# Two attention layers and two expert layers on one core: the first loads in another order, and the values' bias behind the projection of the values

## The chip, the core and the metric

The kernel runs on one core of one Trainium2 chip. What counts is the device time of one execution in microseconds (us). A core has TensorE (PE, matrix products), VectorE (DVE), ScalarE (ACT), GpSimd (POOL) and SyncE (SP, which here only issues transfers), and 16 DMA engines that serve the transfers which SP, ACT and POOL issue. Each engine works through its own list of instructions in order.

## The reference

Four sequences of 1024 tokens with 256 channels go through four residual stages:

```python
x = x + attn0(layernorm(x))   # causal, 16 heads of 16, linear position bias
x = x + ffn0(layernorm(x))    # router, 2 of 4 experts, each a full attention
x = x + attn1(layernorm(x))   # causal, rotary positions
x = x + ffn1(layernorm(x))    # 8 of 64 experts, and a shared one
...
qkv = x @ w_attn + b_attn     # in attn0
y = softmax(scores) @ v
return y @ w_proj + b_proj
```

Each row of the softmax sums to one, so the bias of v goes through it unchanged: the kernel leaves that bias out of v and adds b_v @ w_proj + b_proj, one row of 256 numbers, to x beforehand.

## The kernel before

All of x stays in SBUF, as four tiles x0 to x3 of 128 partitions x 8 x 256 floats (1 MB each; token 128 i + p lies in partition p). Everything is float32.

**The first attention** (`layer0_attn`) makes one job for each sequence and gives them to `run_attention`, which writes the order of PE, DVE and ACT out by hand, tick by tick. A job has `prepare` (the normalisation `norm`), `make_qk` (queries and keys of a group of four heads), `values` (`project_v`) and `finish`. A tick makes one step of the maxima: two score products (L282), the causal mask on the diagonal (L294) and the maximum (L297); later ticks also make a step of exponentials (L317, L328) and of products with v (L385). Between them the running parts get a turn each; that is how `values` lies among the first steps of maxima. For the first sequence `norm` comes first: 8 statistics (L76, L77), reciprocal root (L81 to L85), shift (L87), 8 row blocks on POOL (L98), 16 transposes on PE (L109), two copies on ACT (L113). Then pq and pk (L165), qa (L634) and ka (L639), which needs bk and the constant kc; then the steps of maxima begin.

**The bias** (`out_bias`): two loads on SP, bcol (1 KB, L200) and brow (128 KB, L204); a copy that spreads bcol (brep, L202); two products with wo (pbias, L207); the sum with brow (L211). `add_bias` (L217, POOL) adds the result to a whole x tile. Before, `out_bias` is called ahead of the jobs, so pbias is the first thing PE does, and `add_bias` is the last thing in `prepare`.

**The loads at the start.** SP: x0 in one transfer, gw and its second part (the last layer's gates, L1068, L1071), wq, wk, wv, wo (L593), bq, bk (L611, L612), bcol, brow, kc (L616); then `ffn_constants`: four small ones, four fills of the memory that the first expert layer gathers in (xc, 4 MB each, L690), neg (L712); then the first expert's weights and bias. ACT: x1, x2, x3. A transfer takes one of eight semaphores in turn, and SP waits, before it issues one, for the transfer that had the same semaphore. The scaling of bq (L613) stands in DVE's list ahead of the shift (L87).

Of the kernel before, what the change touches and what calls it, by code (L numbers as in the profile page):

```python
# [16 lines left out]
ALU = mybir.AluOpType  # L17
# [4 lines left out]
P = 128  # L22
B, T, C = 4, 1024, 256
# [3 lines left out]
NT = T // P  # L27
NTOK = B * T
E0 = 4
E1, TOPK, CAP = 64, 8, 128  # L30
# [14 lines left out]
class Kernel:  # L45
    def __init__(self, ctx, tc, ins, out):
        self.tc, self.nc, self.ins, self.out = tc, tc.nc, ins, out
        nc = self.nc
        self.const = ctx.enter_context(tc.tile_pool(name="const", bufs=1))
        self.xpool = ctx.enter_context(tc.tile_pool(name="x", bufs=1))  # L50
        self.npool = ctx.enter_context(tc.tile_pool(name="xnT", bufs=2))
        self.small = ctx.enter_context(tc.tile_pool(name="small", bufs=2))

        self.sent = []
        self.x = []
        self.xnT_of = {}
        for b in range(B):
            t = self.xpool.tile([P, NT, C], F32, tag=f"x{b}", name=f"x{b}")
            queue = nc.scalar if b else nc.sync
            queue.dma_start(out=t, in_=ins["x"][b].rearrange("(i p) c -> p i c", p=P))  # L60
            self.x.append(t)
        self.ident = self.const.tile([P, P], F32, tag="ident", name="ident")
        make_identity(nc, self.ident)
        self.z = self.const.tile([P, NTOK // P], F32, tag="z", name="z")

# [534 lines left out]
    def layer0_attn(self):  # L602
        tc, nc, ins = self.tc, self.nc, self.ins
        wp, rp = self.w1, self.r1
        wq = self.load_w(wp, "wq", ins["a_wq"], 512)
        wk = self.load_w(wp, "wk", ins["a_wk"], 512)
        wv = self.load_w(wp, "wv", ins["a_wv"], C)
        wo = self.load_w(wp, "wo", ins["a_wo"], C)
        bq = rp.tile([P, NG], F32, tag="a_bq", name="bq")
        bk = rp.tile([P, NG], F32, tag="a_bk", name="bk")  # L610
        nc.sync.dma_start(out=bq, in_=ins["a_bq"])  # L611
        nc.sync.dma_start(out=bk, in_=ins["a_bk"])  # L612
        nc.vector.tensor_scalar(bq, bq, 0.25, None, ALU.mult)  # L613
        bias = self.out_bias(rp, "a_bias", ins["a_bv"], ins["a_bo"], wo)
        kc = self.p2.tile([P, T], F32, tag="kc", name="kc")
        nc.sync.dma_start(out=kc, in_=ins["pos_rows"])  # L616
        self.ffn_constants()
        jobs = []
        for b in range(B):
            def prepare(job, b=b):  # L620
                yield from self.norm(b, self.ps, self.new_rows())
                job["xnT"] = self.xnT_of[b]
                self.add_bias(b, bias)

            def values(job):
                job["v"] = self.next_v()
                yield from self.project_v(wv, job["xnT"], job["v"])

            def make_qk(job, g):
                qa = self.qk.tile([P, T], F32, tag="qa", name="qa")  # L630
                ka = self.qk.tile([P, T], F32, tag="ka", name="ka")
                job["qk", g] = qa, ka
                pq = self.project(wq, g, job["xnT"], "pq")
                nc.scalar.activation(  # L634
                    qa, pq, AF.Identity, bias=bq[:, g : g + 1], scale=0.25
                )
                yield
                pk = self.project(wk, g, job["xnT"], "pk")
                nc.vector.scalar_tensor_tensor(  # L639
                    ka, pk, bk[:, g : g + 1], kc, ALU.add, ALU.add  # L640
                )
                yield

            def finish(job, b=b):
                yield from self.project_out(job["y"], wo, self.add_to_x(b))

            jobs.append(dict(n=NT, prepare=prepare, make_qk=make_qk, values=values, finish=finish))
            jobs[b]["then"] = self.route0(b) if b else self.route_and_fill()
        self.run_attention(jobs, causal=True)
# [403 lines left out]
    def open_moe(self, ctx):  # L1053
        tc, nc, ins = self.tc, self.nc, self.ins
        wp = self.moe = ctx.enter_context(tc.tile_pool(name="m1", bufs=1))
        dram = ctx.enter_context(tc.tile_pool(name="dm", bufs=1, space=DRAM))

        self.xs = [
            dram.tile([NSLOT + n * T * TOPK, XW], F32, tag=f"xs{k}", name=f"xs{k}")
            for k, n in enumerate((B - 1, 1))  # L1060
        ]

        self.sums = [
            dram.tile([(B - 1) * T + CAP, C], F32, tag=f"sum{k}", name=f"sum{k}") for k in range(2)
        ]
        self.xn_d = [dram.tile([P, 2, T], F32, tag=f"xn{b}", name=f"xn{b}") for b in range(B - 1)]
        self.gw = wp.tile([P, 2, E1 + 1], F32, tag="gw", name="gw")
        nc.sync.dma_start(  # L1068
            out=self.gw[:, :, 0:E1], in_=ins["g_w"].rearrange("(c p) e -> p c e", p=P)
        )  # L1070
        nc.sync.dma_start(  # L1071
            out=self.gw[:, :, E1 : E1 + 1], in_=ins["sg_w"].rearrange("(c p) e -> p c e", p=P)
        )
        self.before = wp.tile([P, P], F32, tag="before", name="before")
        nc.gpsimd.memset(self.before, 1.0)
        nc.gpsimd.affine_select(
            self.before, self.before, pattern=[[1, P]], compare_op=ALU.is_gt, fill=0.0, base=0,
            channel_multiplier=-1,
        )
        self.allones = wp.tile([P, P], F32, tag="allones", name="allones")  # L1080
        nc.gpsimd.memset(self.allones, 1.0)

        self.first = wp.tile([P, E1], F32, tag="first", name="first")
        nc.gpsimd.iota(
            self.first, pattern=[[CAP, E1]], base=1, channel_multiplier=0,
            allow_small_or_imprecise_dtypes=True,
        )
        self.full = wp.tile([1, 1], I32, tag="full", name="full")
        self.counts = wp.tile([P, NT + 1, E1], F32, tag="counts", name="counts")
        nc.vector.memset(self.counts[:, NT, :], 0.0)  # L1090

    def temporary(self, name):
        return self.got.tile([P, 2, C], F32, tag="g", name=name).rearrange(
            "p k c -> p (k c)"
        ).rearrange("p (i e) -> p i e", e=E1)
# [486 lines left out]
```

## Time and profile before

| | us |
|---|---|
| median of 3 runs | 4618.35 |
| the three runs | 4598.04, 4618.35, 4621.28 |
| the profiled execution | 4602.72 |
| its span | 4600.9 |
| PE busy | 4294.8 (93%) |
| DVE busy | 2601.6 (57%) |
| ACT busy | 1941.7 (42%) |
| POOL busy | 629.3 (14%) |
| x0, from issue to landing | 7.4 |
| median of a fill of xc, from issue to landing | 27.8 |

The profile follows one execution. Busy times overlap, since the engines work beside each other, so their sum is no time; what counts is which wait ends last at a place. In a line of the timeline the first number is the start, the second the duration, then come engine, line and operation, the tile written and the tiles read, and in brackets how long the engine stood idle before it and what ended that. SPq and ACTq are issues of transfers, which take time of the issuing engine and say nothing yet of the landing.

### The profile page before, as it was taken

The numbers are of one execution on the slowest core, as the hardware profiler recorded it, in microseconds if no ns is written. First come the engines' busy times: TensorE is split into PE (matmuls) and PEld (weight loads), VectorE is DVE, ScalarE is ACT, GpSimd is POOL, SyncE is SP. The second block draws the span as 40 slices with busy tenths as digits, with TensorE's granted clock in tenths as the row PEclk, the third lists the DMA queues.
The fourth block names the chain that finished last, engine by engine and source line by source line (L and its number), as shares of the span: only waits on it lengthen the run. The fifth ranks groups of instructions, "written<-read, shape, count | busy, mean of one in ns | idle before, by whom it ended". The sixth has DMA issues, their size and how long they took to land.

```text
span 4600.9 us, 85874 instructions
## 1 busy us (share of the span) xinstructions
PE 4294.8 (93%) x36762; PEld 2011.7 (44%) x36762; DVE 2601.6 (57%) x4327; ACT 1941.7 (42%) x4134; POOL 629.3 (14%) x671
## 2 busy tenths in 40 slices
PE   7999999979999998899999999998999998999998
PEld 3444444444444444544434343434334344443556
DVE  5656666636555563455465656563665766657232
ACT  2444444434555553344354555453243333334431
POOL 1002020110000000000000101010210342425243
PEclk8999999989999999999899999999899999999999
DMA  6004000010000000100000100000000111112586
GB/s 218 1 1 142 1 20 4 29 39 1 15 8 8 1 17 30 34 16 18 23 9 10 32 9 20 6 22 28 19 1 28 39 56 41 60 44 86 140 190 174
DMA packets 134443, 188.74 MB, mean 41 GB/s; under 512 B 14816, under 2 KB 116448, under 8 KB 133216
## 3 DMA queue, kind: packets, MB, share of 16 engines
q1 hardware_dynamic: 91584, 99.11, 6.9%
q0 software_dynamic: 27264, 66.18, 5.1%
q10 hardware_dynamic: 15136, 17.20, 1.1%
q8 instruction: 303, 4.96, 0.5%
q14 instruction: 156, 1.28, 0.1%
HBM read 83.36 MB, written 99.09 MB: 40 GB/s over the span
## 4 chain that ended last, share of the span: by engine, by line
PE 51%; issue 17%; DVE 5%; ACT 2%; DMA 1%; POOL 1%; another core or an unknown queue 0%; POOLq 0%; SPq 0%; DVEq 0%; ACTq 0%
PE s L282 16%; PE av L385 9%; PE s L317 6%; PE pa L165 3%; PE pb L165 2%; PE pgu L1263 2%; PE pq L165 2%; PE pk L165 2%; PE po L436 2%; PE pv L182 1%; DVE mx L297 1%; DMA xg<-xs 1%; ACT e L328 1%; PE py L403 1%; PE po L1281 1%
## 5 line engine op out<-in xcount | busy, mean ns | idle before, releaser
L328 ACT ACTIVATE e<-s 128x512 f32<-128x512 f32 (+3 forms) x3428 | 1531.0, 498 | 1829.0 <-PE s L317 1016.0
L297 DVE TENSOR_REDUCE mx<-s 128x2 f32<-128x1024 f32 (+3 forms) x1760 | 1721.8, 981 | 745.8 <-PE s L317 624.7
L317 PE MATMUL s<-qa,ka 32*128 32x384 f32 (+3 forms) x7040 | 1858.7, 552 | 24.5 <-ACT e L328 8.3
L282 PE MATMUL s<-ka,qa 32*128 32x384 f32 (+3 forms) x7040 | 1686.7, 563 | 97.0 <-DVE mx L297 38.8
L385 PE MATMUL av<-e,v 128*32 128x192 f32 (+2 forms) x12800 | 906.2, 359 | 5.6 <-ACT e L334 4.2
L282 PEld LDWEIGHTS s<-ka,qa 32*128 32x128 f32 x7040 | 556.0, 190 | 713.2 <-issue 443.4
L317 PEld LDWEIGHTS s<-qa,ka 32*128 32x128 f32 x7040 | 706.3, 186 | 131.9 <-ACT e L328 76.1
L385 PEld LDWEIGHTS av<-e,v 128*32 128x32 f32 x12800 | 266.6, 109 | 710.9 <-issue 673.0
L294 DVE TENSOR_TENSOR s<-s,mask 128x256 f32<-128x256 f32 x512 | 219.0, 428 | 205.7 <-PE s L282 197.4
L953 POOL DMA_DIRECT2D xc<-os x24 | 18.1, 754 | 2031.4 <-DVE os L949 1872.2
L1241 POOL DMA_INDIRECT xs<-rowsx,dest x192 | 185.7, 967 | 185.2 <-DVE dest L1240 163.0
L341 PEld LDWEIGHTS <-ident_b 128*32 128x32 bf16 x4096 | 62.1, 95 | 231.9 <-issue 217.4
L98 POOL TENSOR_SCALAR rows<-x,rstd,shift 128x256 f32<-128x256 f32 x96 | 51.8, 554 | 767.5 <-DVE shift L87 748.3
L403 PE MATMUL py<-ident,avs 128*128 128x128 f32 x544 | 95.9, 292 | 64.0 <-ACT avs L399 62.7
L341 PE MATMUL s<-mask_kq,ident_b 128*32 128x128 bf16 x4096 | 151.6, 228 | 0.0
L165 PE MATMUL pq<-xT,wq 128*128 128x512 f32 (+2 forms) x384 | 147.4, 522 | 2.6 <-ACT xT L920 2.5
L165 PE MATMUL pk<-xT,wk 128*128 128x512 f32 (+2 forms) x384 | 141.4, 505 | 0.1
L436 PE MATMUL po<-wo,yT 128*128 128x256 f32 x544 | 129.7, 390 | 10.6 <-ACT yT L431 10.6
L941 DVE SCALAR_TENSOR_TENSOR ka<-pk,bk,kc 128x768 f32<-128x768 f32 (+3 forms) x64 | 52.3, 818 | 149.4 <-PE pk L165 149.4
L407 DVE RECIPROCAL rec<-py 128x16 f32<-128x16 f32 (+2 forms) x160 | 38.4, 240 | 164.9 <-PE py L403 164.7
L365 DVE TENSOR_TENSOR qa<-pm,qa 128x512 f32<-128x512 f32 (+2 forms) x160 | 97.4, 609 | 52.8 <-PE pm L361 51.7
L1410 POOL DMA_INDIRECT sum<-ye,idx x64 | 100.0, 1563 | 153.7 <-DVE ye L1408 92.9
(202 smaller groups left out, 3260.0 us busy)
## 6 DMA issues: line engine op xcount, KB each, us to landing
xc<-empty SPq DMA_DIRECT2D x4, 4096.0 KB, 27.8
gu<-in_e_gu SPq DMA_DIRECT2D x64, 256.0 KB, 3.8
xs<-empty ACTq DMA_DIRECT2D x16, 642.0 KB, 6.1
xg<-xs SPq DMA_DIRECT2D x64, 160.5 KB, 3.6
dn<-in_e_dn SPq DMA_DIRECT2D x64, 128.0 KB, 2.4
sum<-sum SPq DMA_DIRECT2D x12, 512.0 KB, 4.8
rows<-xc SPq DMA_DIRECT2D x19, 256.0 KB, 3.1
xc<-os POOLq DMA_DIRECT2D x8, 512.0 KB
```

The costliest lines, as they stand in the source:

```text
L165: nc.tensor.matmul(pt[:, h, 0:wd], lhsT=w[:, c, g * P : (g + 1) * P], rhs=xnT[:, c, h * 512 : h * 512 + wd], start=(c == 0), stop=(c == 1),)
L282: nc.tensor.matmul(s[:, jj, 0:w], lhsT=qa[r : r + 32, q0 : q0 + P], rhs=ka[r : r + 32, k0 : k0 + w], start=True, stop=True,)
L294: nc.vector.tensor_tensor(d, d, self.mask.unsqueeze(1).to_broadcast([P, 2, P]), ALU.add)
L297: nc.vector.tensor_reduce(mx, s[:, :, 0:w], AX.X, ALU.max)
L317: nc.tensor.matmul(t[:, 0 : end - q0], lhsT=ka[r : r + 32, kt * P : (kt + 1) * P], rhs=qa[r : r + 32, u["q0"] + q0 : u["q0"] + end], start ...
L328: lambda e=e, t=t, jj=jj, w=end - q0: nc.scalar.activation(e[:, jj, 0:w], t[:, 0:w], AF.Exp)
L341: nc.tensor.matmul(t[j : j + 32, 0:P], lhsT=self.ident_b[:, j : j + 32], rhs=self.mask_kq, start=False, stop=True, skip_group_check=True,)
L385: nc.tensor.matmul(u["av"][32 * j : 32 * j + 32, c0:c1], lhsT=v[:, kt, c : c + 32], rhs=e[:, j % 2, c0 - q0 : c1 - q0], start=(first and h ...
L403: nc.tensor.transpose(pt[:, q].rearrange("p h r -> p (h r)"), avs[:, q * P : (q + 1) * P], self.ident)
L436: nc.tensor.matmul(po[:, q, :], lhsT=yT[:, q, c, :], rhs=wo[:, c, :], start=(c == 0), stop=(c == 1),)
L1241: d = nc.gpsimd.indirect_dma_start(out=self.xs[int(last)][:, :], out_offset=bass.IndirectOffsetOnAxis(ap=at, axis=0), in_=rows[:, i, :], i ...
L1410: nc.gpsimd.indirect_dma_start(out=of[:, :], out_offset=bass.IndirectOffsetOnAxis(ap=idx[:, 0:1], axis=0), in_=ye, in_offset=None, compute ...
```

## The change

x0 is loaded in four pieces of two row blocks each, by turns on SP and ACT; x1 to x3 are issued on SP, x1 after the attention's weights, x2 and x3 after the constants of the expert layer with their fills. bq and bk go ahead of wq and wk, kc ahead of wv and wo, the two loads of gw behind x3. The scaling of bq is in the first job's `prepare`, behind `norm`. `out_bias` is called in the first job's `values`, behind `project_v`, and its two loads are issued there; `add_bias` is there too, for every sequence. Nothing else differs in what is computed.

```diff
         for b in range(B):
             t = self.xpool.tile([P, NT, C], F32, tag=f"x{b}", name=f"x{b}")
-            queue = nc.scalar if b else nc.sync
-            queue.dma_start(out=t, in_=ins["x"][b].rearrange("(i p) c -> p i c", p=P))
+            if b == 0:
+                for r in range(0, NT, 2):
+                    queue = nc.scalar if r % 4 else nc.sync
+                    queue.dma_start(out=t[:, r : r + 2], in_=self.rows_of(b, r, 2))
             self.x.append(t)
...
+    def rows_of(self, b, i, n):
+
+        return self.ins["x"][b][i * P : (i + n) * P, :].rearrange("(i p) c -> p i c", p=P)
...
-        wq = self.load_w(wp, "wq", ins["a_wq"], 512)
-        wk = self.load_w(wp, "wk", ins["a_wk"], 512)
-        wv = self.load_w(wp, "wv", ins["a_wv"], C)
-        wo = self.load_w(wp, "wo", ins["a_wo"], C)
+
         bq = rp.tile([P, NG], F32, tag="a_bq", name="bq")
         bk = rp.tile([P, NG], F32, tag="a_bk", name="bk")
         nc.sync.dma_start(out=bq, in_=ins["a_bq"])
         nc.sync.dma_start(out=bk, in_=ins["a_bk"])
-        nc.vector.tensor_scalar(bq, bq, 0.25, None, ALU.mult)
-        bias = self.out_bias(rp, "a_bias", ins["a_bv"], ins["a_bo"], wo)
+        wq = self.load_w(wp, "wq", ins["a_wq"], 512)
+        wk = self.load_w(wp, "wk", ins["a_wk"], 512)
         kc = self.p2.tile([P, T], F32, tag="kc", name="kc")
         nc.sync.dma_start(out=kc, in_=ins["pos_rows"])
+        wv = self.load_w(wp, "wv", ins["a_wv"], C)
+        wo = self.load_w(wp, "wo", ins["a_wo"], C)
+        nc.sync.dma_start(out=self.x[1], in_=self.rows_of(1, 0, NT))
         self.ffn_constants()
-        jobs = []
+        for b in range(2, B):
+            nc.sync.dma_start(out=self.x[b], in_=self.rows_of(b, 0, NT))
+        self.load_gates()
+        jobs, biases = [], []
         for b in range(B):
             def prepare(job, b=b):
                 yield from self.norm(b, self.ps, self.new_rows())
                 job["xnT"] = self.xnT_of[b]
-                self.add_bias(b, bias)
-
-            def values(job):
+                if b == 0:
+                    nc.vector.tensor_scalar(bq, bq, 0.25, None, ALU.mult)
+
+            def values(job, b=b):
                 job["v"] = self.next_v()
                 yield from self.project_v(wv, job["xnT"], job["v"])
+                if b == 0:
+                    biases.append(self.out_bias(rp, "a_bias", ins["a_bv"], ins["a_bo"], wo))
+                self.add_bias(b, biases[0])
```

`load_gates` holds the two loads of gw that stood in `open_moe`, unchanged.

More of the change, by code (lines that the diff above doesn't have):

```diff
@@ L1067, in open_moe @@
         self.gw = wp.tile([P, 2, E1 + 1], F32, tag="gw", name="gw")
[L1068 to L1073, printed above, removed]
         self.before = wp.tile([P, P], F32, tag="before", name="before")
@@ L1090, in open_moe, with load_gates @@
         nc.vector.memset(self.counts[:, NT, :], 0.0)
+    def load_gates(self):
+        nc, ins = self.nc, self.ins
+        nc.sync.dma_start(
+            out=self.gw[:, :, 0:E1], in_=ins["g_w"].rearrange("(c p) e -> p c e", p=P)
+        )
+        nc.sync.dma_start(
+            out=self.gw[:, :, E1 : E1 + 1], in_=ins["sg_w"].rearrange("(c p) e -> p c e", p=P)
+        )
     def temporary(self, name):
```

## The prediction

> **What bounds the kernel now.** I read the page first, for the scale and for the chain that ended last; then the timeline of the first 100 us, since every edit lies there; then the transfers' issues and landings; then the table of stretches, for DMA rates and the clock.
>
> ```profile
> span 4600.9 us, 85874 instructions
> ...
> PE   7999999979999998899999999998999998999998
> ...
> DMA  6004000010000000100000100000000111112586
> ...
> PE 51%; issue 17%; DVE 5%; ACT 2%; DMA 1%; POOL 1%; another core or an unknown queue 0%; POOLq 0%; SPq 0%; DVEq 0%; ACTq 0%
> ```
>
> PE works nearly everywhere, and DMA is 1% of the chain. Only the first slice (115 us) shows PE at 7 and DMA at 6. What the change can move lies in that slice; behind it everything follows from PE's and VectorE's own order, so a shift of the start stays a shift of the end.
>
> The timeline of the start (start us, duration us, engine, line):
>
> ```profile
> 8.22 0.43 DVE L76 BATCH_NORM_STATS2 st<-x 128x6 f32<-128x256 f32 x1 [6.13 <-DMA x<-in_x]
> ...
> 16.43 0.43 SPq L200 DMA_DIRECT2D bcol<-in_a_bv  x1
> ...
> 18.94 0.17 DVE L613 TENSOR_SCALAR bq<-bq 128x4 f32<-128x4 f32 x1 [5.70 <-DMA bq<-in_a_bq]
> 19.02 0.16 DVE L87 SCALAR_TENSOR_TENSOR shift<-mv,rstd 128x8 f32<-128x8 f32 x1
> ...
> 19.29 0.32 DVE L202 COPY brep<-bcol 128x256 f32<-128x256 f32 x1
> ...
> 19.65 2.07 PE L207 MATMUL pbias<-wo,brep 128*128 128x256 f32 x4 [19.65 <-DVE brep L202]
> ...
> 20.71 34.38 SPq L690 DMA_DIRECT2D xc<-empty  x4
> ...
> 21.76 0.42 DVE L211 TENSOR_TENSOR bias<-pbias,brow 128x256 f32<-128x256 f32 x1 [2.16 <-PE pbias L207]
> ...
> 44.09 0.43 DVE L294 TENSOR_TENSOR s<-s,mask 128x256 f32<-128x256 f32 x1
> ...
> 55.13 10.67 SPq L712 DMA_DIRECT2D neg<-in_neg_rows  x1
> ```
>
> Two things. VectorE stands from 13.2 to 18.94 at the scaling of bq (L613), and the normalisation's shift is queued behind it: a true loss of the start. And once the four fills of xc are in SP's queue, SP is kept in issuing until 65.8 us.
>
> Whether a small load behind the fills gets past them:
>
> ```profile
> L690 SPq DMA_DIRECT2D xc<-empty x1: 13714/13714/13714, 41.4 to 41.4; - x1
> DMA to landing us min/median/max: 30.6/30.6/30.6
> ...
> neg<-in_neg_rows SPq DMA_DIRECT2D x1, 0.5 KB, 17.6
> ```
>
> The last fill lands at 41.4 + 30.6 = 72.0, and neg, 0.5 KB, at 55.1 + 17.6 = 72.7. It does not get past.
>
> Rates and clock (PE, PEld, DVE, ACT, POOL busy, then clock, DMA share, GB/s):
>
> ```profile
> 0.00:5.00 5.00, 0.00 (x0) 0.00 (x0) 1.08 (x3) 0.00 (x0) 4.35 (x12) 1.00 0.51 167
> 5.00:10.00 5.00, 0.00 (x0) 0.00 (x0) 1.68 (x7) 1.28 (x1) 3.72 (x13) 1.00 1.09 370
> 10.00:15.00 5.00, 0.00 (x0) 0.00 (x0) 2.80 (x13) 0.21 (x1) 0.00 (x0) 1.00 1.07 393
> ...
> 30.00:40.00 10.00, 7.79 (x35) 5.37 (x34) 3.00 (x5) 1.01 (x1) 0.00 (x0) 1.00 1.04 345
> 40.00:50.00 10.00, 8.40 (x37) 3.97 (x37) 6.48 (x10) 1.01 (x1) 0.00 (x0) 0.89 1.04 345
> 50.00:60.00 10.00, 8.26 (x30) 3.09 (x27) 6.92 (x11) 0.00 (x0) 0.00 (x0) 0.50 1.04 344
> ```
>
> Loads run at 370 to 393 GB/s, fills at 345; from the fifties on PE has half its clock.
>
> **The change, part by part.** *The front.* x0 in four pieces over two queues, with nothing of x1 to x3 beside it: x0 (1.05 MB) needs 167 x 5 = 0.84 MB up to 5 us and the rest at 370, so it is there at 5.6, plus about 0.5 to land; the first two pieces, 0.52 MB, at about 4.4. Eight pairs L76/L77 take 4.35 us (8.22 to 12.56): done at 8.8 instead of 12.6. bq now comes before wq and is scaled behind the shift, so the 5.7 us wait goes: ident_b's copy, root and reciprocal as before (0.6), shift at 9.5 instead of 19.02. Without pbias (L207) ahead of the transposes another 1.0 goes. Pool's iota ends at 8.72, wq and wk (1.05 MB behind x0) are in by 9, kc, wv and wo by 12: none is late for a first pq near 13.6. Bound: if PE's clock warms later, 2 us less. The same point in the work comes 8.5 to 10.5 us earlier; I take 10.5.
>
> *What is moved behind.* The built order of the changed kernel differs on PE by one move only: pbias now stands behind the third score step (the first group's projections, three score steps and the 16 value products are ahead of it), with the copy brep and the sum bias at that place on VectorE. Queued behind on VectorE: the mask of the fourth step, all maxima, the ka of all later groups. On PE: all scores. Nothing of either can pass. The third maximum ends near 44.0 - 10.5 = 33.5.
>
> brep waits for bcol. L200's two loads no longer stand at 16.43, before the fills, but on SP behind: four fills, neg, x2, x3, and the two loads of gw. So:
> - ahead of the fills: x0, wq, wk, kc, wv, wo, x1 = 4.19 MB. By the table 0.84 + 1.85 = 2.69 MB by 10 us, the other 1.50 at 393: 13.8. Four small loads behind x1: 1.0 (estimate; they are issued 0.47 apart now). Fills start at 14.8, were issued about 11 and so wait in the queue.
> - fills: 16.78 MB at 345 = 48.6: until 63.4.
> - x2 and x3: 2.10 MB at 380 = 5.5: 68.9.
> - gw, its second part, bcol, in small pieces: 1.2 (estimate, from wo and the small bcol behind it landing 0.2 apart to gw landing 0.9 after x0); landing: 1.4 of the 2.8 us that bcol took alone. bcol is there at 71.5.
> - Issue isn't later: neg's ends 6.2 us before the last fill lands, so near 57; x2, x3 and gw at most 4 each (the third x on ACT's queue took 3.76), bcol by 66 to 69.
>
> Bounds: 68.5 with no price for small pieces and landing, 75 if the fills get 325 GB/s.
>
> From landing to the next mask, by the rows above: bcol there 19.2, brep, pbias, bias done 22.2, so 3.0; the fourth step's two score products behind pbias add 0.3. The fourth mask stands at 44.09 now, and at 71.5 + 3.3 = 74.8 then: **+30.7**. VectorE and PE idle from 33.5 to 71.5; the 10.5 won at the front only lengthen that idling, and are worth nothing.
>
> *The clock behind the wait.* A few rows of PE:
>
> ```profile
> 46.72 1.13 PE L282 MATMUL s<-ka,qa 32*128 32x512 f32 x4 [0.42 <-DVE mx L297]
> 48.05 3.75 PE L282 MATMUL s<-ka,qa 32*128 32x512 f32 x8 [0.20 <-DVE mx L297]
> ...
> 68.40 5.28 PE L165 MATMUL pq<-xnT,wq 128*128 128x512 f32 x8
> ...
> 74.89 3.70 PE L165 MATMUL pk<-xnT,wk 128*128 128x512 f32 x8 [0.36 <-ACT qa L634]
> ```
>
> A 512-wide step goes from 1.13 to 1.88 us at 48, and full speed is back only within pq (5.28 against 3.70): some 23 us at half clock, although PE was busy 8 to 9 tenths. The Trainium skill (TensorE: Matmul & The Clock Gate, "What's actually happening") says that an idle window of about 3.4 us halves the clock and one busy window of that length restores it. After 38 us of idling both agree on a cold start. By the rule it lasts one window, about +1 us; then the steps up to pq, cold from 48 on today, would be quicker than now by about 0.45 us in each of some 13, -6: 30.7 + 0.3 + 1 - 6 = +26. By the row, score products on 32 rows do not restore it, and only pq does: then the four steps that are warm today (256, 384, 384 and 512 wide: 0.9, 1.24, 1.33, 1.33) cost 1.28, 1.57, 1.57 and 1.88 as the cold ones do: +1.5. I take the row.
>
> *The rest.* brep of the first expert stands one step later on VectorE, waiting for its bcol, 1.7 MB of weights behind: 4.8 us after ours, when VectorE arrives at 4.7. 0 to 2; I take 0.3. add_bias (4.51 us on POOL) runs near 75 instead of 24.3, with POOL idle until 197 now: nothing, hidden while x0's attention lasts. x1 is in at 14, x2 and x3 at 69, and their rows are made at 197, 326 and later; gw is used in the last layer; nothing. ACT issues two transfers less: its root waits for rstd anyway; nothing.
>
> Sum: 30.7 + 1.5 + 0.3 = **+32.5 us**. On the profiled execution's own 4602.72 (span 4600.9 and 1.8 around it) that is 4635.2. It was one of the quicker ones: the three timed runs and it have their middle at (4602.72 + 4618.35) / 2 = 4610.5. I put the sum on that: **4643**.
>
> **The rivals.**
> - *The bias' load is not held (not slower).* Were bcol's 1 KB served beside the fills, it would be there before 33.5; 10.5 won, 2.5 paid for pbias and bias at their new place: -8, 4602.5. It decides from a landing before about 62, where the loss is 23 us, 0.5%. For it: nothing but bcol's size. Against it: neg, smaller, landed 0.7 us behind the last fill, and brep's own wait cannot be passed in order. 5%.
> - *The clock comes back at once* (the rule above): +26, 4636.5. For it: the idle start is followed by PE working without gaps. Against: the same steps stayed cold for 20 us now. 20%.
> - *A longer wait*: fills at 325 GB/s (+3), the second brep 2 us late, pq and pk cold for another window (+3): +40, 4650.5. For it: two pieces of the wait are estimates. 15%.
> - The forecast: 60%.
>
> **How the numbers follow.** Apart from the first rival the cases reach from +23 (clock back at once, bcol at 68.5) to +40; runs of one kernel lie up to 12 us off their middle: 4610.5 + 23 - 12 to 4610.5 + 40 + 12 gives 4622 to 4662, which leaves out the first rival and the ends. About 0.5%, 23 us, is what a measurement of this kernel can tell from no change. Slower by more: the forecast, the longer wait, and half or more of the clock rival, less what the spread of runs takes: 0.78. Within: the first rival and the rest: 0.20. Faster: 0.02.
>
> **What would show it.** In the changed profile: shift (L93 there) near 9.5; brep (L208) on VectorE with some 38 us of idling put down to bcol, ending near 71.5; the last fill landing near 64; half clock from there to the next pq near 100; POOL's add_bias near 75; the steps behind 120 us as now, all later by one amount. It is wrong if bcol lands before the fills' end, or if the score steps behind the wait run at 1.3 us and not at 1.6 to 1.9.

## The result, and the profile after

| | before | after |
|---|---|---|
| median, us | 4616.61 (6 runs, 4598.04 to 4621.35) | 4648.93 (6 runs, 4640.81 to 4658.39) |
| the profiled execution | 4602.72, span 4600.9 | 4640.81, span 4639.1 |

The ratio after/before is 1.0076, with a 95% interval of 1.006 to 1.0091: slower by 32.3 us between the medians, where +32.5 was forecast (4643, range 4622 to 4662). The page of the changed kernel:

```profile
span 4639.1 us, 85876 instructions
...
PE   5999999979999998899999999998999999999998
...
PEclk7999999988999999999899999999899999999999
DMA  6003100000000001100000000000000111112586
...
PE 65%; DVE 5%; ACT 3%; issue 2%; DMA 2%; POOL 1%; SPq 0%; DVEq 0%; ACTq 0%; POOLq 0%
```

PE's first slice (116 us) is 5 instead of 7: about a quarter of that slice is lost there, and no other slice has lost as much. PE's rise in the chain from 51% to 65% is no loss of time: the chain now goes through PE's own work where before it put 17% down to issue, and PE's busy time grew by only 17 us (4294.8 to 4312.0).

The timeline of the start after the change (start, duration, engine, line; in brackets the idle time before and what ended it):

```profile
4.35 0.43 DVE L82 BATCH_NORM_STATS2 st<-x 128x6 f32<-128x256 f32 x1 [2.26 <-DMA x<-in_x]
...
9.41 0.17 DVE L93 SCALAR_TENSOR_TENSOR shift<-mv,rstd 128x8 f32<-128x8 f32 x1
...
34.30 0.69 DVE L303 TENSOR_REDUCE mx<-s 128x2 f32<-128x512 f32 x1
```

The front does what it says: the shift stands at 9.41 instead of 19.02. The third maximum ends at 34.99; before, it ended at 44.00 (43.31 + 0.69). Of 9.6 us won, 9.0 are left there. VectorE from there on, first in the kernel before, then in the changed one:

```profile
43.31 0.69 DVE L297 TENSOR_REDUCE mx<-s 128x2 f32<-128x512 f32 x1
...
78.63 1.28 DVE L639 SCALAR_TENSOR_TENSOR ka<-pk,bk,kc 128x1024 f32<-128x1024 f32 x1 [2.63 <-PE pk L165]
```

```profile
69.27 0.29 DVE L208 COPY brep<-bcol 128x256 f32<-128x256 f32 x1 [34.27 <-DMA bcol<-in_a_bv]
71.73 0.42 DVE L217 TENSOR_TENSOR bias<-pbias,brow 128x256 f32<-128x256 f32 x1 [2.17 <-PE pbias L213]
72.96 0.43 DVE L300 TENSOR_TENSOR s<-s,mask 128x256 f32<-128x256 f32 x1 [0.81 <-PE s L288]
...
74.37 2.58 DVE L208 COPY brep<-bcol 128x256 f32<-128x256 f32 x1
...
111.47 1.28 DVE L652 SCALAR_TENSOR_TENSOR ka<-pk,bk,kc 128x1024 f32<-128x1024 f32 x1 [2.63 <-PE pk L171]
```

One bracket holds the result: VectorE stood 34.27 us for bcol, and the fourth mask came at 72.96 instead of 44.09, **+28.9 us**. The last line is the keys of the second group, at 78.63 before: **+32.8**. Another 4.0 us were lost between the two. They begin at the second copy, which took 2.58 us where the first took 0.29.

Who waits for whom, from the table of waits of the first 120 us (sum, number, longest):

```profile
PE pbias L213 <- DVE brep L208: 35.8, 1, 35.8
DVE brep L208 <- DMA bcol<-in_a_bv: 34.3, 1, 34.3
```

PE waits for VectorE, and VectorE for the transfer. Why bcol came so late shows in the issues on SP (duration of the issue in ns, its start in us; below it the time from issue to landing), here the last fill, neg and the bias' bcol:

```profile
L703 SPq DMA_DIRECT2D xc<-empty x1: 12175/12175/12175, 32.3 to 32.3; - x1
DMA to landing us min/median/max: 30.3/30.3/30.3
...
L725 SPq DMA_DIRECT2D neg<-in_neg_rows x1: 12048/12048/12048, 44.6 to 44.6; - x1
DMA to landing us min/median/max: 18.6/18.6/18.6
...
L206 SPq DMA_DIRECT2D bcol<-in_a_bv x1: 636/636/636, 64.1 to 64.1; - x1
DMA to landing us min/median/max: 5.2/5.2/5.2
```

The last fill lands at 32.3 + 30.3 = 62.6, neg at 63.2, bcol at 69.3: one after the other, in the order of their issue. The issue of neg (0.5 KB) alone kept SP for 12 us, and bcol was not issued before 64.1. The stretches (PE, PEld, DVE, ACT, POOL busy, clock, DMA share, GB/s):

```profile
40.00:50.00 10.00, 0.00 (x0) 0.00 (x0) 0.00 (x0) 0.00 (x0) 0.00 (x0) 0.50 1.04 345
...
60.00:70.00 10.00, 0.39 (x1) 0.39 (x2) 0.29 (x1) 0.00 (x0) 0.00 (x0) 0.50 1.04 316
...
90.00:100.00 10.00, 9.27 (x28) 3.10 (x24) 7.04 (x9) 0.00 (x0) 0.00 (x0) 0.50 0.00 0
100.00:110.00 10.00, 9.64 (x20) 3.77 (x19) 2.78 (x4) 2.40 (x2) 0.00 (x0) 0.72 0.00 0
```

All five engines stand at zero while the fills flow at 345 GB/s. PE's last product ends at 33.79, the granted clock falls to half at 37.2, and it is still at half from 90 to 100, where PE is busy 9.27 of 10. Some rows of PE there, then POOL's, first in the changed kernel and then before:

```profile
74.27 1.65 PE L288 MATMUL s<-ka,qa 32*128 32x384 f32 x4 [0.98 <-DVE mx L303]
77.96 3.41 PE L288 MATMUL s<-ka,qa 32*128 32x512 f32 x8 [2.04 <-DVE mx L303]
...
100.20 6.32 PE L171 MATMUL pq<-xnT,wq 128*128 128x512 f32 x8
...
107.73 3.70 PE L171 MATMUL pk<-xnT,wk 128*128 128x512 f32 x8 [0.36 <-ACT qa L647]
```

```profile
72.30 4.50 POOL L223 TENSOR_TENSOR x<-x,bias 128x2048 f32<-128x2048 f32 x1 [57.69 <-DVE bias L217]
...
230.01 4.31 POOL L104 TENSOR_SCALAR rows<-x,rstd,shift 128x256 f32<-128x256 f32 x8 [153.22 <-DVE shift L93]
```

```profile
24.30 4.51 POOL L217 TENSOR_TENSOR x<-x,bias 128x2048 f32<-128x2048 f32 x1
197.18 4.30 POOL L98 TENSOR_SCALAR rows<-x,rstd,shift 128x256 f32<-128x256 f32 x8 [168.36 <-DVE shift L87]
```

PE is back at full speed only within pq, at 105.5. POOL's addition ends at 76.80, and the long copy on VectorE at 74.37 + 2.58 = 76.95, right behind it. The rows of the second sequence start at 230.01, 197.18 before: again +32.8. So the loss is complete by the second group and is only carried on from there. The spans differ by 38.2; the rest of 5.4 us is spread over the later stages, where matching stretches differ both ways (143.0 us at clock 0.93 before, 137.4 at 0.98 after; 2328.0 at 0.97 before, 2332.2 at 0.96 after). The medians differ by 32.3.

### The profile page after: what moved, and what is told of

It is laid out like the page before. It is cut to its first block, busy times and chain, and to the rows that moved or that the text cites. A ratio compares the mean times of both kernels' runs of the same rounds, so it can differ in the third digit from the quotient of the medians.

```text
span 4639.1 us, 85876 instructions
## 1 busy us (share of the span) xinstructions
PE 4312.0 (93%) x36762; PEld 2015.8 (43%) x36762; DVE 2603.8 (56%) x4327; ACT 1942.0 (42%) x4134; POOL 629.0 (14%) x671
## 4 chain that ended last, share of the span: by engine, by line
PE 65%; DVE 5%; ACT 3%; issue 2%; DMA 2%; POOL 1%; SPq 0%; DVEq 0%; ACTq 0%; POOLq 0%
PE s L288 21%; PE av L391 12%; PE s L323 8%; PE pq L171 3%; PE pk L171 3%; PE pa L171 3%; PE pb L171 2%; PE pv L188 2%; PE po L442 2%; PE pgu L1279 2%; DVE mx L303 2%; DMA xg<-xs 1%; PE py L409 1%; PE pm L367 1%; ACT e L334 1%
```

## The experiments

**The theory**: brep stands in order on VectorE, and its bcol is held in SP's queue behind 16.8 MB of fills. **Rivals**: any small load is slow while fills take the bandwidth, whatever its queue; the moved products and the copy cost the time at their new place; the new order of the loads costs it. A second theory followed from the after-trace: the last 4.0 us are the copy held by POOL's addition, and the cold clock. The ratios are to the kernel before on the same chip; its median was 4611.09, 4687.17, 4614.69 and 4674.71 on four of them, so medians are not compared across chips.

**1. The bias' loads first.** Two helpers, load_bcol and load_brow, hold the two loads of `out_bias`, which takes what is loaded already. Experiments 2, 3, 5, 6, 7 and 10 have them too.

```diff
         wo = self.load_w(wp, "wo", ins["a_wo"], C)
+        early = self.load_bcol(ins["a_bv"]), self.load_brow(ins["a_bo"])
...
-                    biases.append(self.out_bias(rp, "a_bias", ins["a_bv"], ins["a_bo"], wo))
+                    biases.append(self.out_bias(rp, "a_bias", ins["a_bv"], ins["a_bo"], wo, early))
```

> The changed kernel with bcol and brow loaded ahead of x1 and the fills; everything else in its order. Theory A (the loss is the wait of the copy brep for bcol, which stands in SP's queue behind the fills): brep starts near 34 us instead of 69, the fourth mask near 37; the first expert's bcol is still behind the fills (near 76) and its copy stands on VectorE where about 73 is reached, so some 3 us stay lost: about 5 us under before, 4612. Rival B (pbias and the bias at their new place, among the steps, cost the time): still 20 us or more over before. Rival C (the fills' traffic itself slows the start, wherever bcol stands): unchanged, 4649.

Measured: 4601.57 (before 4611.09), ratio 0.9979 [0.997, 0.9988]. The copies on VectorE:

```profile
33.58 0.28 DVE L219 COPY brep<-bcol 128x256 f32<-128x256 f32 x1
...
79.05 0.28 DVE L219 COPY brep<-bcol 128x256 f32<-128x256 f32 x1
```

No bracket: no wait. With the products and the first copy at the changed kernel's place, the whole loss is gone and 9.5 us are won; the keys of the second group stand at 72.04 (before 78.63). So neither the moved products nor the new order costs the time. The second copy, for which a loss of some 3 us was expected, lost nothing. It is not at the changed kernel's place: in this build it stands behind the keys of the second group in VectorE's list, as in the kernel before (80.97), well behind POOL's addition and behind its load. Its place differs from build to build: right behind the bias' sum in 2, 3, 5, 6, 7 and 10, and where the changed kernel has it, between the fifth mask and its maximum, in 4, 8, 11 and 12.

**2. The first expert's load early too.**

```diff
+        self.first_bcol = self.load_bcol(ins["f_bv"][0])
```

> As the first, with the first expert's bcol ahead of the fills too. A: no wait of VectorE for a transfer is left, about 8 us under before, 4609. B: 20 us or more over before. C: 4649.

Measured: 4604.06, ratio 0.9985 [0.9975, 0.9994]; keys of the second group at 70.97. It is no better than the first: with no second wait there was nothing to save.

**3. Bias at the front, as before, with the new order of loads.**

```diff
+        bias = self.out_bias(rp, "a_bias", ins["a_bv"], ins["a_bo"], wo)
+        self.first_bcol = self.load_bcol(ins["f_bv"][0])
...
+                self.add_bias(b, bias)
...
-                    biases.append(self.out_bias(rp, "a_bias", ins["a_bv"], ins["a_bo"], wo))
-                self.add_bias(b, biases[0])
```

> As the second, with the bias computed ahead of the jobs again, so that pbias is PE's first work: the order of the loads alone. A: about 9 us under before, 4608, within 2 us of the second. B: 9 us under before as well, but 25 us or more quicker than the second. C: 4649.

Measured: 4603.15, ratio 0.9987 [0.9979, 0.9995]. bcol's copy waited until 12.73, so pbias held the transposes until 14.95; the keys of the second group stand at 73.23, 1.2 later than in experiment 1. The intervals of 1 and 3 overlap: whether the move itself is worth that 1.2 us is not settled. One row of VectorE is worth keeping for later:

```profile
17.07 3.25 DVE L708 TENSOR_SCALAR bq<-bq 128x16 f32<-128x16 f32 x1 [1.26 <-DMA bq<-in_f_bq]
```

A scaling of 16 numbers took 3.25 us and ended at 20.32, beneath POOL's addition, 15.77 to 20.30.

**4. The bias behind the values alone**, in the kernel before, with its old order of loads.

```diff
-        bias = self.out_bias(rp, "a_bias", ins["a_bv"], ins["a_bo"], wo)
...
-                self.add_bias(b, bias)
...
+                if b == 0:
+                    biases.append(self.out_bias(rp, "a_bias", ins["a_bv"], ins["a_bo"], wo))
+                self.add_bias(b, biases[0])
```

> The kernel before, with the bias behind the projection of the values and nothing else: x0 in one piece, x1 to x3 on ACT, gw first, the old order of weights. bcol then stands behind the fills and neg. A: bcol near 73, fourth mask near 77 against 44.1, colder steps +1.5, the second copy up to 3: +36, 4652, more than the whole change. If the new order of loads were the cause: within 3 us of before, 4617. B: +20 or more, but with brep at its place near 44 and no wait for a transfer.

Measured: 4641.16, ratio 1.007 [1.0056, 1.0083]. Half of the change makes the whole loss:

```profile
70.42 0.29 DVE L202 COPY brep<-bcol 128x256 f32<-128x256 f32 x1 [26.96 <-DMA bcol<-in_a_bv]
...
77.44 1.01 DVE L202 COPY brep<-bcol 128x256 f32<-128x256 f32 x1 [1.83 <-DMA bcol<-in_f_bv]
```

The wait is 7.3 us shorter than in the changed kernel and ends within 1.2 us of the same time. This shows that the front's gain goes into the wait. (By the ratio the loss is 32 us; 36 were expected.)

**5. The loads at their new place, on ACT's queue instead of SP's.** The first expert's load is early here and in 6, 7 and 10.

```diff
+                    early = (self.load_bcol(ins["a_bv"], nc.scalar),
+                             self.load_brow(ins["a_bo"], nc.scalar))
```

> The changed kernel with bcol and brow issued at the same place of the program, near 34 us, while the fills are in full flow, but on ACT's queue; the first expert's bcol ahead of the fills, so that no second wait is left. Theory A (order within SP's queue): bcol lands some 3 to 6 us after its issue, brep near 38, fourth mask near 42, about 3 us under before, 4608. Rival C (all the DMA engines are taken by the fills, whatever the queue): brep near 65 to 70, 4640 or more.

Measured: 4684.6 (before 4687.17), ratio 1.0002 [0.9988, 1.0016]. The issue on ACT, then the copy on VectorE:

```profile
31.99 0.37 ACTq L203 DMA_DIRECT2D bcol<-in_a_bv  x1
```

```profile
37.83 0.29 DVE L219 COPY brep<-bcol 128x256 f32<-128x256 f32 x1 [4.05 <-DMA bcol<-in_a_bv]
```

Issued in the midst of the fills (338 GB/s from 30 to 40 us), bcol is used 5.8 us later. The rival of bandwidth would have it wait to the sixties. What held it was SP's queue. In the changed kernel it landed 5.2 us after its issue at 64.1, so most of its wait lay ahead of that issue; the experiment takes away SP's held issue and the place behind the fills together, and does not tell them apart. What is left, a wait of 4.05 us, takes back most of the gain.

**6. Half of the fills behind the bias' loads.**

```diff
-            nc.sync.dma_start(
-                out=self.xc[b].rearrange("(i p) c -> p i c", p=P),
-                in_=zeros.unsqueeze(1).to_broadcast([P, E0 * NT, C]),
-            )
+        self.fill_half(0)
...
                     biases.append(self.out_bias(rp, "a_bias", ins["a_bv"], ins["a_bo"], wo))
+                    self.fill_half(1)
```

> The changed kernel with half of each fill (8.4 MB of 16.8) issued behind bcol and brow, and the first expert's bcol ahead of all. A: the wait shrinks by the fills' own time, 24.3 us: brep near 45 instead of 69.3, fourth mask near 49 against 44.1 before, and PE restarts cold: 4 to 7 us over before, 4616. B (the new place costs): 20 us or more over before. C: 4645 or more.

Measured: 4697.8 (before 4687.17), ratio 1.0019 [1.0005, 1.0033], +8.9 us by the ratio.

```profile
48.47 0.29 DVE L219 COPY brep<-bcol 128x256 f32<-128x256 f32 x1 [14.01 <-DMA bcol<-in_a_bv]
```

The fourth mask comes at 52.16, +8.1. The expectation was some 3 us too low.

**7. The first expert's load early, nothing else**: `self.first_bcol` as in 2, the bias' loads as in the changed kernel.

> The changed kernel with the first expert's bcol alone ahead of the fills: the second wait of VectorE (2.3 us at 74.4 in the changed kernel's profile) taken away and the first left. A: brep still near 69.5, 2 us under the changed kernel, 30 over before, 4641. If the two waits were one cost, and the second copy the one that counts: 4610 to 4620.

Measured: 4716.63 (before 4687.17), ratio 1.0068 [1.0047, 1.0089].

```profile
71.48 0.29 DVE L219 COPY brep<-bcol 128x256 f32<-128x256 f32 x1 [37.22 <-DMA bcol<-in_a_bv]
...
74.28 0.28 DVE L219 COPY brep<-bcol 128x256 f32<-128x256 f32 x1
```

The second copy now stands just ahead of POOL's addition (74.52) and takes its 0.28 us. From the first copy to the keys of the second group it is 39.0 us (110.52), against 42.2 in the changed kernel. The medians cannot show a gain of this size: the intervals of the two ratios overlap.

**8 and 9. PE kept busy through the wait**, by 9 and 11 rounds of a projection that nobody reads, ahead of `out_bias`; one run each.

```diff
+                    for _ in range(11):
+                        self.project(wq, 0, job["xnT"], "keep")
```

> The changed kernel with 36 more projections of 128x512 on PE ahead of pbias (results unused), some 33 us that fill the wait, so that PE's clock is full when bcol comes near 69.3. The clock by the row (score steps on 32 rows lose it and do not restore it, as in the kernel before): pbias takes 1.1 instead of 2.1, the first steps run at 1.3, then half clock comes back some 24 us after the dense work's end or sooner and stays until the next pq; pq begins 1 to 3 us sooner than in the changed kernel, near 98. By the skill's rule (a busy window restores the clock, an idle one takes it): full clock for all steps, pq near 94. If the clock had no share in the loss: pq at 100.2 as before.

With 9 rounds the products ended at 64.73, PE stood 6.18 us, and pbias was cold again (2.07 us): 4730.78 on the chip of 4687.17. It tells nothing of the clock.

> As the run with 36 more projections on PE (their results unused), with 44, some 38 us, so that they end where bcol lands and leave no gap of 6 us ahead of pbias. By the row: pbias takes 1.1 instead of 2.1, one to three score steps run at full clock, then half clock until the next pq; from brep's start to the first pk some 1 to 3 us less than the 38.5 of the changed kernel. By the skill's rule: the score steps keep full clock and that stretch takes 32 us or less. If the clock had no share: 38.5.

With 11 rounds: 4642.96 on the chip of 4614.69. They reach pbias:

```profile
71.85 1.03 PE L213 MATMUL pbias<-wo,brep 128*128 128x256 f32 x4
...
76.20 1.13 PE L288 MATMUL s<-ka,qa 32*128 32x512 f32 x4 [0.42 <-DVE mx L303]
77.53 2.07 PE L288 MATMUL s<-ka,qa 32*128 32x512 f32 x4 [0.20 <-DVE mx L303]
...
98.18 5.15 PE L171 MATMUL pq<-xnT,wq 128*128 128x512 f32 x8
```

The same four products take 1.13 and, one step later, 2.07 us. The clock kept warm fell to half at 77.2, 4.4 us after pbias ended (72.88), though PE was not idle for over 1.13 us at a time; in these 4.4 us it was busy 64%. It stayed at half for 24 us, with PE busy 87% up to pq, and came back within pq, at 101.1. From the first copy to pk it is 33.6 us, against 38.5 in the changed kernel, where 1 to 3 us less were expected. Of these 4.9, 1.7 are the second copy (0.84 us here, beneath the end of POOL's addition), 1.2 are pq, which differs from run to run without such a cause (see below), and 2.0 are the warm products and steps ahead of pq.

**10. All fills behind the bias' loads.**

```diff
                     biases.append(self.out_bias(rp, "a_bias", ins["a_bv"], ins["a_bo"], wo))
+                    self.fill_half(0)
+                    self.fill_half(1)
```

> The changed kernel with all four fills issued behind bcol and brow, the first expert's bcol ahead: the bias and its loads stay where the change has put them. A: with no fill ahead bcol is there before VectorE asks for it: brep near 34 with no wait, the ratio to before 0.998 to 0.9985 as with the loads moved ahead, and on one line with half (brep 48.5) and all of the fills (71.5 on that chip) ahead. B: 0.5% over before or more. C (the fills' traffic): no gain over before either, since the same 16.8 MB flow beside the first steps.

Measured: 4605.51 (before 4614.69), ratio 0.9982 [0.9971, 0.9994].

```profile
33.67 0.28 DVE L219 COPY brep<-bcol 128x256 f32<-128x256 f32 x1
```

With 0, 8.4 and 16.8 MB of fills ahead (10, 6 and 7) the first copy stands at 33.7, 48.5 and 71.5. The fills, still running at 368 GB/s from 30 to 40 us here, disturb nothing when they are behind.

**11. The addition later**, by six empty turns ahead of `add_bias` for the first sequence.

```diff
+                    for _ in range(6):
+                        yield
                 self.add_bias(b, biases[0])
```

> The changed kernel with POOL's addition of the bias to x0 some turns later (the part of the values yields six times ahead of it), so that it no longer runs while VectorE copies the first expert's brep; everything else in its order. If POOL's addition is what stretched that copy from 0.3 to 2.6 us (theory of the second loss): the copy takes 0.3, the steps behind it come 2 us sooner, ratio to before near 1.007. If the copy waited for its bcol: it stays at 2.6 or shows as idling of VectorE, ratio unchanged at 1.0076. The first wait stays in both: brep near 69 to 71.

The addition came at once all the same (74.05 to 78.55), as soon as the bias was there. The second copy took 2.58 us and ended at 78.70:

```profile
76.12 2.58 DVE L208 COPY brep<-bcol 128x256 f32<-128x256 f32 x1
```

It is in effect the changed kernel again: 4700.87 (before 4674.71), ratio 1.0052 [1.0034, 1.0069].

**12. No addition to the first sequence**, one run. It leaves out the bias of that sequence.

```diff
-                self.add_bias(b, biases[0])
+                if b:
+                    self.add_bias(b, biases[0])
```

> The changed kernel without POOL's addition of the bias to x0 (the first sequence goes on without it); the copies, pbias and the bias are made as before. If POOL's addition stretched the copy of the first expert's brep: it takes 0.3 us instead of 2.6, and from the first brep's start to the start of the first group's second ka (42.2 us in the changed kernel) it is some 2 us less, near 40. If the copy was held by its transfer or by anything else: it stays at 2.6 and 42.2.

4633.5, beside 4602.4 for the kernel before. The fourth mask and the second copy on VectorE, then pq on PE:

```profile
73.73 0.43 DVE L300 TENSOR_TENSOR s<-s,mask 128x256 f32<-128x256 f32 x1 [0.81 <-PE s L288]
...
75.13 0.28 DVE L208 COPY brep<-bcol 128x256 f32<-128x256 f32 x1
```

```profile
98.67 5.45 PE L171 MATMUL pq<-xnT,wq 128*128 128x512 f32 x8
```

The copy stands at the same place behind the same masks, and takes 0.28 instead of 2.58 us. From the first copy to the keys of the second group it is 39.0 us, against 42.2. From the fourth mask to pq it is 24.9, as in experiments 1 and 7, against 27.2 in the changed kernel and 24.3 before: the addition costs 2.3 us there, and the cold clock 0.6. The other 0.9 between 39.0 and 42.2 lie in pq, 5.45 us here and 6.32 there. That does not follow the addition: pq took only 4.86 in experiment 8, whose second copy was held too (2.66 us), and 6.43 in experiment 5, whose copy was not.

## Why the prediction was right

- *The front, 10.5 us earlier, worth nothing.* The shift came at 9.41 (9.5 said), the third maximum 9.0 us earlier (10.5 said). The first pq took 4.72 us instead of 3.70, as if PE's clock was not up yet; the rows of the granted clock stand at 1.00 there, so this is read from the durations alone. It differs from run to run: with the same front, pq took 3.60 in experiments 5 and 10, and the third maximum ended at 33.8, 10.2 us earlier than before. It cost nothing, since the wait swallowed the front; experiment 4 against the changed kernel (1.0070 and 1.0076) shows that, and experiment 1 shows what the front is worth without the wait.
- *brep waits for bcol behind the fills.* Right, with its cause: the queue (5) and what is ahead in it (6, 10), not the bandwidth. bcol's copy stood at 69.27, 71.5 was said; the fills ended at 62.6 instead of 63.4, and x2, x3 and the small loads after them were 1.4 us quicker than estimated. The fourth mask: +28.9 instead of +30.7.
- *The clock, +1.5.* The mechanism is right, the size in part by luck: 4.0 less the copy's 2.3 leaves 1.7. The colder steps up to pq, for which the 1.5 was worked out, cost only 0.6 (experiment 12). The other 1.0 is pq's own slower start (6.32 against 5.28 us), which the forecast left as it was (only its longer wait reckons with a colder pq); pq took from 4.86 us (experiments 2 and 8) to 6.43 (experiment 5), so this is scatter between executions. The rule of the Trainium skill (TensorE: Matmul & The Clock Gate, "What's actually happening") that one busy window brings the clock back would have made the total +26; the changed kernel's products ran at half clock from 69.6 until within pq, at 105.5, and experiment 9 shows a warm clock fall in the midst of these products. The measurement decides for the row.
- *The first expert's brep, +0.3, "waiting for its bcol", and POOL's addition "nothing, hidden".* This is the step that failed, though the total did not show it. That load was there at 73.98, before VectorE came (74.37). The copy lost 2.3 us to POOL's addition, which the change put above it. Before, the addition ran from 24.30 to 28.81 with no copy beneath, which is why its price did not show. It is shown by 7 (copy ahead of the addition: 0.28), 12 (no addition: 0.28), and by where the copies end: 76.95 behind 76.80, 78.45 behind 78.30 in experiment 4, 78.70 behind 78.55 in 11. The Trainium skill (SBUF — State Buffer, "Who interferes with whom") states it: VectorE's copies, casts and scalings between SBUF tiles can take the ports that VectorE shares with GpSimd for themselves, and one engine then waits for the other. The rows agree; that it is these ports, no run here shows by itself. The maxima and masks, which read PSUM, ran at their usual length beside the same addition.
- *The sum.* 28.9 + 2.3 + 0.6 + 1.0 = 32.8, as measured at the second sequence's rows: the terms of 30.7, 0.3 and 1.5 were off by -1.8, +2.0 and +0.2, and cancelled. That +32.5 met the difference of the medians to 0.2 us is luck; the two profiled executions differ by 38. The base was 4610.5 and is 4616.6 by six runs, which makes the 6 us between 4643 and 4648.9.
- *The rivals.* "Not held" (-8, 4602.5) is what the kernel would have been with the loads ahead: experiment 1 measured -9.5.

Two things stay open. No run here delays POOL's addition past the copy (11 did not); experiment 1 has no such overlap. And how much of bcol's delay is SP's held issue and how much the order within its queue is not told apart; the order does count, since neg, whose issue ended at 56.6, still landed behind the last fill.

## What to carry to other kernels

Moving a step moves its transfers too: look at what stands ahead of them in the queue where they are now issued. A load that an in-order engine needs early is issued ahead of the bulk transfers of its queue, or on another queue; its size does not help it past them. A gain ahead of a wait for a fixed time is worth nothing until the wait is gone: with two lines of loads moved (experiment 1) the same change went from a ratio of 1.0076 to 0.9979. That is the lowest of all these versions, though the intervals of experiments 1, 2, 3 and 10 overlap.

## What was not expected of the hardware

- An SBUF copy on VectorE that starts beneath a large addition on POOL ended 0.15 us after the addition (2.58 us instead of 0.29 in the changed kernel, and the same 0.15 in experiments 4, 9 and 11). A scaling of 16 columns took 3.25 us and ended 0.02 us after it. Operations that read PSUM went on at their usual length.
- The score products on 32 rows did not bring the clock back, even with PE busy 87% of 21 us (experiment 9), and did not keep it up: full speed lasted 4.4 us behind the last dense products, with PE busy 64% in between. It came back within the next pq, 3.0 us after its start there and 5.3 in the changed kernel. Whether the 32 rows or the short gaps between the steps are the reason, no run here separates.
